# A graph layer with row gathers: 32 single rows per step instead of 40, one register load per engine and block, 43 fillers instead of 42

## The chip, the cores and the metric

The kernel runs on one core of one Trainium2 chip. The metric is the device time of one execution in microseconds (us), median of the runs. The engines are named PE (TensorE, matrix products), DVE (VectorE), ACT (ScalarE), POOL (GpSimd) and SP (SyncE); SP and ACT here also issue transfers (DMAs), and POOL issues the indirect ones that gather rows by a list of indices.

## What is computed

One layer of a graph network over 50,000 nodes of 128 features and 1,650,000 edges, which come sorted by their target `dst`. 50,000 of the edges are self-loops, one for each node.

```
Xs = X[src]
m_data = Xs @ W_data.T + b_data
m_ctrl = Xs @ W_control.T + b_control
msg = where(edge_types == 0, m_data, m_ctrl)
agg = segment_sum(msg, dst, num_segments=N)
out = relu(agg + X @ W_self.T + b_self)
result = layernorm(x + out)
```

Since the products are linear, the kernel first sums the rows `x[src]` of each target and edge type, and multiplies the sums by the weights afterwards. So the large part of the work is to fetch 1,650,000 rows of 512 bytes and to add them up.

## The kernel before

**Blocks and steps.** The edges are cut into `NBLK` blocks, worked through one after the other by a loop over `b` that is unrolled by hand (L614 to L664). A block has `Q = 2` steps, and a step has three kinds of edges:

- `SIZE = 1536` edges in `R = 12` columns of 128, one on each partition. One indirect DMA on POOL (L477) gathers one column: 128 rows. A block has 24 such gathers, in four passes of `PASS = 6`, each with a buffer `y` of its own out of `SLOTS = 10`.
- `F = 42` fillers. Self-loops among the 1,536 need no gather, since their rows lie in the window of node rows `xT` which the block loads anyway. `fill(b)` (L309) finds the first `F` self-loops of the step and puts `F` other edges in their places, so that the same gathers bring `F` more edges. It is all on DVE: comparisons, products and sums over 26 columns x `F` numbers (`m`, `new`, `v_new`, `old`, `by`, L319 to L338). The self-loops that were put out are added back by `left_out_columns`, `left_out_matrix`, `left_out_numbers` and `left_out_rows`. It needs `F` self-loops in each step; `find_bad` (L565) counts them on the chip, and where a step has fewer than `F` a second, general way of computing the whole layer runs after the first (`general`, L667).
- `S = 40` single rows, each fetched by an ordinary DMA of 512 bytes at an address out of a register: `TURNS = (20, 20)`, 20 for each step by SP and 20 by ACT (`single_rows`, L437). `offsets` (L430) has DVE turn indices into byte offsets (`at_x`, L435); a register load (L446) brings them into the engine's registers, `LOADS = 2` loads of 20 registers for each block and engine; then 20 DMAs follow each load (L451).

So a step covers 1,536 + 42 + 40 = 1,618 edges and a block 3,236. The first block takes 3,072 edges without fillers and single rows, then come as many full blocks as fit (508), and the last block takes the rest, 3,040 edges, again by plain gathers alone: 24 of them. That is `NBLK = 510` and 510 x 24 = 12,240 gathers. The last 96 rows are one shorter gather.

**What comes after the gathers.** PE waits for a pass (L484), then multiplies the gathered rows by one-hot matrices (`oh`, L412, with counts `cnt`, L420, from DVE), which adds them up into `acc` (L496). At the end of a step it takes the 40 single rows in one more product (L502), for which it waits in `rows_fetched` (L456). DVE adds `acc` to `sums` (L512), PE multiplies by the weights (`layer`, L527), DVE forms relu, residual and the moments of the norm (L541 to L546), ACT takes the root (`sd`, L551), DVE scales (L557, L559) and SP writes the rows out (L563).

**The order of the work.** Each engine works through its own instructions in the order of the program. Single rows are fetched two blocks ahead (`AHEAD = 2`), fillers five (`RAHEAD = 5`). At block `b`, ACT's order is: load of 20 registers and 20 rows for `b + 2`, the root of block `b - 1`, load and 20 rows for `b + 2`. SP's order is: the window `xT` of `b + 3`, load and 20 rows, load and 20 rows, the writing out of block `b - 1`. At every tenth block SP also loads the edge lists of the next ten (`load_edges`), a group; there are 51 groups. POOL has nothing but the gathers after its first two microseconds.

Of the kernel before, what the change touches and what calls it, by code (L numbers as in the profile page):

```python
# [36 lines left out]
Q = 2  # L37
PASS = 6
B = 112
C = R * Q  # L40
F = 42
TURNS = (20, 20)
S = sum(TURNS)
LOADS = 2
X = Q * S
R1 = R + 1
C1 = Q * R1
SIZES = [P] * R
SIZE = sum(SIZES)
CE = Q * SIZE  # L50
BE = CE + Q * F + X
NBLK = 2 + (E - CE) // BE
REST = E - CE - (NBLK - 2) * BE
REST_ROWS = [min(n, max(0, REST - q * SIZE - sum(SIZES[:r]))) for q in range(Q) for r, n in enumerate(SIZES)]
# [23 lines left out]
TBL = GROUPS * GB  # L78
# [3 lines left out]
def plain(b):  # L82

    return b == 0 or b >= NBLK - 1
# [6 lines left out]
def straight(ctx, tc, c, x, x_t, src_t, dst_t, etype_t, src_f, dst_f, etype_f, src_x, dst_first, first_p, out):  # L91
# [35 lines left out]
                   allow_small_or_imprecise_dtypes=True)  # L127
    FILL = Q * F + C1
    small = keep_ps.tile([P, 2 * W + F + 2 * FILL + 2], F32, name="small")
    num_ps, rank_no_ps = small[:, :2 * W], small[:, 2 * W:2 * W + F]  # L130
    lists = [small[:, 2 * W + F + i * FILL:][:, :FILL] for i in range(2)]
    sums_at = [small[:Q * F, 2 * W + F + 2 * FILL + i:][:, :1] for i in range(2)]

# [29 lines left out]
    def load_edges(g):  # L163
        t = eds.tile([1, GB * X], I32, name="one_g")
        nc.sync.dma_start(t, src_x[None, g * GB * X:(g + 1) * GB * X])
        one_g[g] = t
        loads[g] = {}
        for name, a in (("s", src_t), ("d", dst_t), ("t", etype_t)):
            t = eds.tile([P, GB, C1], I32, name=name, bufs=1)
            nc.sync.dma_start(t.rearrange("p b c -> p (b c)"), a[:, g * GC:(g + 1) * GC])  # L170
            loads[g][name] = t
        for name, a in (("sf", src_f), ("df", dst_f), ("tf", etype_f)):
            t = eds.tile([GS, F], I32, name=name, bufs=1)
            nc.sync.dma_start(t, a[g * GS:(g + 1) * GS, :])
            loads[g][name] = t
# [54 lines left out]
    def check(d, rel, at, name):  # L230
        chk = eds.tile(list(d.shape), F32, name="chk" + name, bufs=1)
        nc.vector.scalar_tensor_tensor(chk, d, float(DST_PAD), rel, op0=ALU.is_lt, op1=ALU.mult)
        axes = AX.XY if len(d.shape) == 3 else AX.X
        nc.vector.tensor_reduce(at[0], chk, axes, ALU.min)
# [74 lines left out]
    def fill(b):  # L309
# [15 lines left out]
        v = fil.tile([P, C1], F32, name="v_new")  # L325
        nc.vector.tensor_reduce(v, new, AX.X, ALU.add)  # L326
        vi = fil.tile([P, C1], I32, name="vi")
# [9 lines left out]
        with nc.allow_low_precision(reason="whole numbers below 256, one of them not 0"):  # L337
            nc.vector.tensor_reduce(by, old.rearrange("p (q r) f -> p q f r", r=R1), AX.X, ALU.add)  # L338
        bys[b] = by
# [76 lines left out]
    def counts(b):  # L416

        cnt = ohp.tile([P, Q, 2 * W], BF16, name="cnt")
        with nc.allow_low_precision(reason="whole numbers up to R1"):
            nc.vector.tensor_reduce(cnt, ohs[b].rearrange("p (q r) w -> p q w r", r=R1), AX.X, ALU.add)  # L420
        cnts[b] = cnt
# [8 lines left out]
    def offsets(b):  # L430

        if not plain(b):
            g, i = divmod(b, GB)
            ats[b] = stp.tile([1, X], I32, name="at_x", bufs=AHEAD + 2)
            nc.vector.tensor_scalar(ats[b], one_g[g][:, i * X:(i + 1) * X], float(ROW), None, op0=ALU.mult)  # L435

    def single_rows(b, part):  # L437

        if part == 0:
            ys[b] = stp.tile([S, Q, D], F32, name="yx", bufs=ROW_SLOTS)  # L440
        both = []
        for j, (eng, dma) in enumerate(((SP, nc.sync), (ACT, nc.scalar))):
            n = Q * TURNS[j]
            k0, k1 = part * n // LOADS, (part + 1) * n // LOADS
            at = Q * sum(TURNS[:j])
            _, rows = nc.values_load_multi_w_load_instructions(ats[b][0:1, at + k0:at + k1], engines=[eng], **RANGE)  # L446
            both.append([(dma, fetched[j][b % ROW_SLOTS], *divmod(k0 + k, TURNS[j]), sum(TURNS[:j]), row)
                         for k, row in enumerate(rows)])
        for pair in zip_longest(*both):
            for dma, sem, q, k, at, row in filter(None, pair):  # L450
                copy = dma.dma_start(ys[b][at + k:at + k + 1, q, :].bitcast(U8), x_bytes[:, bass.ds(row, ROW)])  # L451
                copy.then_inc(sem, 16)
                tc.no_tile_sem_insts.add(copy.ins.name)
                tc.add_to_no_dep_group(f"single{b}", copy.ins)

    def rows_fetched(b):  # L456

        times = len(range(b % ROW_SLOTS or ROW_SLOTS, b + 1, ROW_SLOTS))
        for j in range(2):
            wait = nc.tensor.wait_ge(fetched[j][b % ROW_SLOTS], 16 * Q * TURNS[j] * times)  # L460
        tc.declare_fence(wait.ins, group=f"single{b}")
# [141 lines left out]
    for b in range(1, RAHEAD):  # L603
        fill(b)
        left_out_columns(b)
        left_out_matrix(b)
        if b < AHEAD:
            onehot(b)
            counts(b)
            for part in range(LOADS):  # L610
                single_rows(b, part)
        if b == 1:
            clear_sums()
    for b in range(NBLK + 1):  # L614
# [16 lines left out]
        for q, (step, ks) in enumerate(passes_of(b)):  # L631
# [26 lines left out]
            if q == 3:  # L658
                left_out_matrix(b + RAHEAD)
                offsets(b + AHEAD + 1)  # L660
            if q < LOADS and not plain(b + AHEAD):
                single_rows(b + AHEAD, q)
# [226 lines left out]
def gnn_resnorm(  # L889
# [50 lines left out]
    with ExitStack() as own:  # L940
        straight(own, tc, c, x, x_t, src_t, dst_t, etype_t, src_f, dst_f, etype_f, src_x,
                 dst_first, first_p, out)
# [58 lines left out]
```

## Time and profile before

| | |
|---|---|
| time before, median of 3 runs (lowest, highest) | 15340.11 us (15320.92, 15340.7) |
| the profiled execution's own time | 15323.45 us |
| its span, first to last instruction | 15321.7 us |
| POOL: gathers L477 with `idx` as list, 12,216 of them | 11540.9 us busy, 945 ns each |
| POOL: idle just before them | 3733.3 us |
| DVE busy | 10904.6 us, 71% of the span |
| PE busy (products; weight loads lie beside) | 8296.6 us, 54% |
| ACT busy (without the issuing of DMAs) | 153.6 us, 1% |
| one row's issue on SP or ACT: register move and DMA | 29 and 228 ns, 20,320 times on each |
| a load of 20 registers (L446), median | 1437 ns on ACT, 1378 ns on SP |

How to read it: an instruction's row gives its count, its mean duration, and how long its engine sat idle just before it, with what ended that idle time ("issue" where nothing that the profile shows was waited for). In the timeline each line has the start, the duration, the engine (ACTq, SPq and PEq are the sequencers that issue DMAs and wait), the line of the kernel, the operation and its tiles.

### The profile page before, as it was taken

The numbers are of one execution on the slowest core, as the hardware profiler recorded it, in microseconds if no ns is written. First come the engines' busy times: TensorE is split into PE (matmuls) and PEld (weight loads), VectorE is DVE, ScalarE is ACT, GpSimd is POOL, SyncE is SP. The second block draws the span as 40 slices with busy tenths as digits, with TensorE's granted clock in tenths as the row PEclk, the third lists the DMA queues.
The fourth block names the chain that finished last, engine by engine and source line by source line (L and its number), as shares of the span: only waits on it lengthen the run. The fifth ranks groups of instructions, "written<-read, shape, count | busy, mean of one in ns | idle before, by whom it ended". The sixth has DMA issues, their size and how long they took to land. (4 is left out here: it accounts for less than half of the span.)

```text
span 15321.7 us, 197234 instructions
## 1 busy us (share of the span) xinstructions
PE 8296.6 (54%) x35844; PEld 7096.5 (46%) x35845; DVE 10904.6 (71%) x13994; ACT 153.6 (1%) x516; POOL 11565.0 (75%) x12250
## 2 busy tenths in 40 slices
PE   3555555555555555555555555555555555555555
PEld 3444444444444444444444444444444444444444
DVE  8777777777777777777777777777777777777775
ACT  0000000000000000000000000000000000000000
POOL 7777777777777777777777777777777777777777
PEclk7555555555555555555555555555555555555555
DMA  2222222222222222222222222222222222222222
GB/s 65 62 61 62 61 62 61 62 62 61 62 61 62 61 62 61 62 61 62 62 60 62 61 62 61 62 62 61 61 62 62 61 62 61 62 61 62 62 61 56
DMA packets 649293, 939.07 MB, mean 61 GB/s; under 512 B 327756, under 2 KB 445487, under 8 KB 648034
## 3 DMA queue, kind: packets, MB, share of 16 engines
q0 software_dynamic: 391680, 802.93, 20.9%
q1 hardware_dynamic: 215276, 112.76, 2.9%
q10 hardware_dynamic: 41078, 10.68, 0.3%
q14 instruction: 968, 7.93, 0.2%
q8 instruction: 291, 4.77, 0.1%
HBM read 895.92 MB, written 29.42 MB: 60 GB/s over the span
## 5 line engine op out<-in xcount | busy, mean ns | idle before, releaser
L477 POOL DMA_INDIRECT y<-in_x,idx x12216 | 11540.9, 945 | 3733.3 <-issue 3552.2
L496 PE MATMUL acc<-oh,y 128*128 128x120 f32 x24480 | 5867.6, 429 | 5768.3 <-PEq L484 5767.8
L496 PEld LDWEIGHTS acc<-oh,y 128*128 128x128 f32 x24480 | 5313.7, 326 | 6190.7 <-PEq L484 6178.3
L420 DVE TENSOR_REDUCE cnt<-oh 128x240 bf16<-128x3120 f32 x510 | 2959.6, 5803 | 0.1
L541 DVE COPY h<-po 112x128 f32<-112x128 f32 x510 | 148.7, 292 | 2499.1 <-PE po L535 2407.5
L412 DVE TENSOR_TENSOR oh<-col,small 128x3120 f32<-128x3120 f32 x510 | 1719.5, 3372 | 0.0
L512 DVE TENSOR_TENSOR sums<-acc,sums 128x180 f32 x1020 | 352.2, 345 | 1393.1 <-PE acc L505 1236.0
L338 DVE TENSOR_REDUCE by<-old 128x84 bf16<-128x1092 f32 x508 | 1078.5, 2123 | 17.6
L502 PE MATMUL acc<-oh,yx 40*128 40x120 f32 x2032 | 777.4, 484 | 0.0
L345 PE MATMUL small<-ones_b,by 128*84 128x1 bf16 x508 | 117.4, 231 | 1191.1 <-DVE by L338 1191.1
L319 DVE TENSOR_TENSOR m<-rk,small 128x1092 f32<-128x1092 f32 x508 | 656.4, 1292 | 17.3
L322 DVE TENSOR_TENSOR new<-m,small 128x1092 f32<-128x1092 f32 x508 | 656.2, 1292 | 17.3
L326 DVE TENSOR_REDUCE v_new<-new 128x26 f32<-128x1092 f32 x508 | 655.8, 1291 | 17.3
L345 PEld LDWEIGHTS <-by 128*84 128x84 bf16 x508 | 74.3, 146 | 1267.3 <-DVE by L338 1267.2
L335 DVE TENSOR_TENSOR old<-m,small 128x1092 f32<-128x1092 f32 x508 | 652.3, 1284 | 0.0
L502 PEld LDWEIGHTS acc<-oh,yx 40*128 40x128 f32 x2032 | 497.5, 304 | 210.0 <-issue 205.3
L535 PE MATMUL po<-wmsgT,sums 128*112 128x128 f32 x2040 | 515.1, 396 | 0.0
L535 PEld LDWEIGHTS po<-wmsgT,sums 128*112 128x112 f32 x2040 | 374.0, 253 | 108.2 <-issue 88.7
L533 PE MATMUL po<-bias,sums 3*112 3x128 f32 x1020 | 350.3, 439 | 0.0
L525 DVE TENSOR_TENSOR sums<-pl,sums 128x336 f32<-128x336 f32 x508 | 257.9, 508 | 85.2 <-DVE sums L512 84.6
L532 PE MATMUL po<-wselfT,xT 128*112 128x128 f32 x1020 | 315.5, 412 | 0.0
L551 ACT ACTIVATE sd<-mv,eps 112x1 f32<-112x1 f32 x510 | 150.4, 295 | 15051.3 <-DVE mv L546 8335.5
(118 smaller groups left out, 4174.2 us busy)
## 6 DMA issues: line engine op xcount, KB each, us to landing
yx<-in_x ACTq DMA_DIRECT2D x20320, 0.5 KB
yx<-in_x SPq DMA_DIRECT2D x20320, 0.5 KB
y<-in_x,idx POOLq DMA_INDIRECT x12216
xT<-in_x_t SPq DMA_DIRECT2D x510, 56.0 KB
out<-o SPq DMA_DIRECT2D x510, 56.0 KB
vf_all<-vd SPq DMA_DIRECT2D x51, 420.0 KB
s<-in_src_t SPq DMA_DIRECT2D x51, 130.0 KB
d<-in_dst_t SPq DMA_DIRECT2D x51, 130.0 KB
```

What stands on the lines that cost most here:

```text
L319: nc.vector.tensor_tensor(m, rk_g[g][:, i, :, None].to_broadcast([P, C1, F]), rank_no_ps[:, None, :].to_broadcast([P, C1, F]), op=ALU.is_e ...
L322: nc.vector.tensor_tensor(new.rearrange("p (q r) f -> p q r f", r=R1), m.rearrange("p (q r) f -> p q r f", r=R1), vf.rearrange("p (q f) -> ...
L326: nc.vector.tensor_reduce(v, new, AX.X, ALU.add)
L335: nc.vector.tensor_tensor(old, m, cb[:, :, None].to_broadcast([P, C1, F]), op=ALU.mult)
L338: nc.vector.tensor_reduce(by, old.rearrange("p (q r) f -> p q f r", r=R1), AX.X, ALU.add)
L412: nc.vector.tensor_tensor(oh, col_g[g][:, i, :, None].to_broadcast([P, C1, 2 * W]), num_ps[:, None, :].to_broadcast([P, C1, 2 * W]), op=AL ...
L420: nc.vector.tensor_reduce(cnt, ohs[b].rearrange("p (q r) w -> p q w r", r=R1), AX.X, ALU.add)
L477: copy = nc.gpsimd.indirect_dma_start(out=y[:r, k % PASS, :].bitcast(U8), out_offset=None, in_=x_rows, in_offset=bass.IndirectOffsetOnAxis ...
L496: nc.tensor.matmul(acc[:, :2, :].rearrange("p t w -> p (t w)"), y[:r, k % PASS, :], ohs[b][:r, column(k), :], start=k == of_step[0], stop= ...
L502: nc.tensor.matmul(acc[:, :2, :].rearrange("p t w -> p (t w)"), ys[b][:, q, :], ohs[b][:S, q * R1 + R, :], start=False, stop=True)
L512: nc.vector.tensor_tensor(part, accs.pop((b, q)), part, op=ALU.add)
L535: nc.tensor.matmul(po, a[:, t, :B], c["wmsgT"][:, t * D:(t + 1) * D], start=False, stop=t == 1)
```

## The change

The numbers of single rows, loads and fillers change, and with them the cut of the edges. `BEGIN` is the place in `at_x` where each engine's offsets begin, rounded up to four; `part_of` cuts a block's offsets into `LOADS` parts.

```diff
-F = 42
-TURNS = (20, 20)
+F = 43
+TURNS = (16, 16)
 S = sum(TURNS)
-LOADS = 2
-X = Q * S
+LOADS = 1
+BEGIN = (0, -(-Q * TURNS[0] // 4) * 4)
+X = BEGIN[1] + -(-Q * TURNS[1] // 4) * 4
...
-BE = CE + Q * F + X
+BE = CE + Q * (F + S)
 NBLK = 2 + (E - CE) // BE
...
+    def part_of(n, part):
+
+        return n if part == LOADS else -(-part * n // (4 * LOADS)) * 4
+
     def single_rows(b, part):
...
             n = Q * TURNS[j]
-            k0, k1 = part * n // LOADS, (part + 1) * n // LOADS
-            at = Q * sum(TURNS[:j])
+            k0, k1 = part_of(n, part), part_of(n, part + 1)
+            at = BEGIN[j]
             _, rows = nc.values_load_multi_w_load_instructions(ats[b][0:1, at + k0:at + k1], engines=[eng], **RANGE)
...
-        ones[1:] = np.concatenate([single[:, :, sum(TURNS[:j]):][:, :, :n].reshape(TBL - 1, Q * n)
-                                   for j, n in enumerate(TURNS)], axis=1)
+        for j, n in enumerate(TURNS):
+            ones[1:, BEGIN[j]:BEGIN[j] + Q * n] = single[:, :, sum(TURNS[:j]):][:, :, :n].reshape(TBL - 1, Q * n)
```

A step now covers 1,536 + 43 + 32 = 1,611 edges and a block 3,222. That makes 511 full blocks instead of 508, `NBLK = 513`, and leaves 486 edges for the last block: four gathers, the last of 102 rows. For each full block, SP and ACT now issue one load of 32 registers and 32 rows each, all of them ahead of ACT's root of the block before (with `LOADS = 1`, L661 calls `single_rows` at the first pass alone). `S = 32` rows enter the product L502 instead of 40. The groups become 52.

## The prediction

> **What bounds the kernel now.** I read the page's first parts to see which engine has least room, then the groups of instructions for that engine, then the timeline of one block for what its gaps are. The page:
>
> ```profile
> PE 8296.6 (54%) x35844; PEld 7096.5 (46%) x35845; DVE 10904.6 (71%) x13994; ACT 153.6 (1%) x516; POOL 11565.0 (75%) x12250
> ...
> L477 POOL DMA_INDIRECT y<-in_x,idx x12216 | 11540.9, 945 | 3733.3 <-issue 3552.2
> L496 PE MATMUL acc<-oh,y 128*128 128x120 f32 x24480 | 5867.6, 429 | 5768.3 <-PEq L484 5767.8
> L496 PEld LDWEIGHTS acc<-oh,y 128*128 128x128 f32 x24480 | 5313.7, 326 | 6190.7 <-PEq L484 6178.3
> ```
>
> No engine is above 75%, yet POOL's busy time and the idle time just before its gathers make 11540.9 + 3733.3 = 15274.2 us of the 15321.7. 3552.2 us of that idle time is "issue", a gap in which POOL waited for nothing shown: 0.30 us after every gather. PE's largest idle time is the wait for gathered rows (L484). So POOL issues gathers back to back, and everything else follows it. The timeline of one block, some lines of it:
>
> ```profile
> 7517.97 14.49 SPq L451 DMA_DIRECT2D yx<-in_x  x40
> ...
> 7518.98 0.95 POOL L477 DMA_INDIRECT y<-in_x,idx  x1 [0.30 <-issue]
> ...
> 7524.73 0.29 ACT L551 ACTIVATE sd<-mv,eps 112x1 f32<-112x1 f32 x1 [29.59 <-DVE mv L546]
> ...
> 7526.31 28.88 ACTq L451 DMA_DIRECT2D yx<-in_x  x40
> ...
> 7531.47 0.94 POOL L477 DMA_INDIRECT y<-in_x,idx  x1 [0.30 <-issue]
> ...
> 7533.96 0.94 POOL L477 DMA_INDIRECT y<-in_x,idx  x1 [0.30 <-issue]
> ...
> 7536.44 0.15 DVE L557 RECIPROCAL rstd<-sd 112x1 f32<-112x1 f32 x1
> ...
> 7546.41 0.26 DVE L435 TENSOR_SCALAR at_x<-one_g 1x80 int32<-1x80 int32 x1
> 7546.45 0.95 POOL L477 DMA_INDIRECT y<-in_x,idx  x1 [0.30 <-issue]
> ```
>
> Two things are to be seen. First, ten gathers lie between 7518.98 and 7531.47 and ten between 7533.96 and 7546.45: 1.249 us each in both stretches. In the first SP and ACT are issuing rows all the time; in the second they issue none. (ACT's line of 28.88 us merges two batches. The first ends near 7526.31 + 20 x 0.317 = 7532.7, as a row takes 0.317 us: 29 + 228 ns and two gaps of some 30. The second can't begin before `at_x` is written at 7546.67.) Second, SP and ACT stand idle for some 14 of the block's 30 us: the queues of the single rows bound nothing.
>
> The whole run agrees with this. The first gather, the first after the start-up, and the last:
>
> ```profile
> 3.21 1.12 POOL L477 DMA_INDIRECT y<-in_x,idx  x1 [1.09 <-DMA idx<-in_src_t]
> ...
> 85.50 0.94 POOL L477 DMA_INDIRECT y<-in_x,idx  x1 [3.19 <-PE acc L496]
> ...
> 15305.30 0.92 POOL L477 DMA_INDIRECT y<-in_x,s  x1 [0.30 <-issue]
> ```
>
> The one at 85.50 is the 61st, since POOL has buffers for 10 x 6 gathers and here waits for PE to free the first. From it to the last, the 12,240th, are 12,179 intervals in 15219.80 us: 1.2497 us each, 29.99 us per block of 24.
>
> **The change part by part.**
>
> *More gathers: +65.0 us, on the path.* Three more full blocks and a last block of four gathers instead of 24 make 24 + 511 x 24 + 4 = 12,292 gathers, 52 more. At 1.2497 us each that is 64.98 us. This is the cost of dropping 16 single rows per block: the rows that SP and ACT fetched beside POOL's work are now gathered by POOL. One more filler per step gives back only two of the sixteen.
>
> *Fewer rows and one load on SP and ACT: 0 on the path.* Per block and engine 8 rows x 0.317 = 2.5 us are saved, in queues that are idle for 14 us. What hides any cost is that idle time and, for the rows themselves, the two blocks between fetch and use. In the order of the work one thing moves: ACT's root now comes after 32 rows instead of 20, so 12 x 0.317 = 3.8 us later, plus what a load of 32 registers takes beyond one of 20. The trace has no load of 32. Bounds: nothing more than the 1.44 us of 20 registers (SP's five-register load L400 has a median of 1.29, so the number hardly counts there), or two loads of 20, 1.44 more. I take 0.9, 12 registers at 1.44/20 each. The root ends 3.8 to 5.3 us later. Behind it on DVE waits L557. In this block the root was done at 7524.73 + 0.29 = 7525.02 and L557 began at 7536.44, because the counts (L420, 5.8 us) come before it: 11.4 us of cover. Were the cover gone, DVE would stall and the writing out would be late, and only then, through `acc` and `sums`, PE and POOL's buffers. On SP all rows are issued in one batch and end earlier than the second batch of 20 did; the writing out L563 behind them waits for DVE anyway.
>
> The Trainium skill speaks against the longer load: "Runtime: NRT & Kernel Launch", section "Instruction fetch mechanics", puts a register load at about 200 ns per register. The row here says 72 ns (1437 / 20). By the page, 32 registers would take an estimated 6.4 us, the root would come some 8.8 us later, still within the 11.4, and the sum would stay the same.
>
> *43 fillers: +0.17 us of DVE per block, hidden; +0.7 us once.* L319, L322, L326, L335 and L338 go from 26 x 42 = 1,092 to 1,118 elements. Together they take 1292 + 1292 + 1291 + 1284 + 2123 = 7282 ns, and 26/1092 of it is 0.17 us. DVE waits per block 2499.1 / 510 = 4.9 us before L541 and 1393.1 / 510 = 2.7 before the 2 x L512, which covers it. At the start it isn't covered: four fills come one after the other before PE's first products, and the wait at 85.50 ends on them (PE's L345 at 82.20 waits for the fourth fill's L338, and L496 follows it): 4 x 0.17 = 0.7 us.
>
> *The end: +4.6 us.* Before, the last block's 24 gathers hid the previous block's layer. With four gathers (5 us) they don't. Lines of the end before:
>
> ```profile
> 15277.97 2.92 PE L496 MATMUL acc<-oh,y 128*128 128x120 f32 x12 [4.45 <-PEq L484]
> ...
> 15283.78 0.39 DVE L523 COPY sums<-sums 128x336 f32 x1 [0.16 <-DVE sums L512]
> ...
> 15307.88 2.92 PE L496 MATMUL acc<-oh,y 128*128 128x120 f32 x12 [4.33 <-PEq L484]
> ...
> 15313.44 0.29 DVE L541 COPY h<-po 112x128 f32<-112x128 f32 x1 [2.16 <-PE po L535]
> ...
> 15315.22 0.34 DVE L559 TENSOR_SCALAR o<-h,mv,rstd 112x128 f32<-112x128 f32 x1
> ```
>
> From the last gather's start at 15305.30: products begin 2.6 us later, and L559 ends at 10.3. After the change: products of the last four gathers from 2.6 to 4.5 (two thirds of 2.9), counts to 4.9, then the previous block's layer (2.7 us, L531 to L535 here) to 7.6, its moments, root and scaling (2.1 us, 15313.44 to 15315.56) to 9.8, the last `acc` into `sums` to 10.5, the bias and weight products that need it (2.1) to 12.7, moments, root and scaling (2.1) to 14.9: 4.6 us more. Bounds: 0, if these stages overlap fully, and 6, the previous block's layer, moments and scaling in full with the last `acc`.
>
> One more group (the ten-block loads) costs what it costs in the 1.2497 already. Sum: 15323.45 + 65.0 + 0.7 + 4.6 = 15393.8 us against the profiled execution. Two of the three runs shown, and the median, lie 17 us above that execution (15340.11 to 15323.45); with the same distance the median after is 15340.1 + 70.3 = 15410 us, 0.46% more. From the lowest run it would be 15391.
>
> **The rivals.**
>
> *Fewer row issues make POOL's gathers shorter, so that it is not slower.* For it: the rows share memory and DMA engines with the gathers, and 0.30 of every 1.25 us is an unexplained gap. Against: the two stretches above, 1.249 with and without rows. To cancel 70 us, the 12,231 intervals after the start-up would have to shrink by 5.7 ns, to 1.244; that is the shortest gather (940 ns, against 944 in the median) with its gap of 0.30. At 1.240 for all, the median would be 15410 - 12231 x 0.0097 = 15291 us.
>
> *Something late reaches POOL.* A root, or rows, later than their cover. It decides from 11.4 us of extra lateness at ACT's root on; each microsecond per block that gets through costs 511 us, so one would give 15,920. Against it: 3.8 to 5.3.
>
> *The second, general computation runs.* `find_bad` asks for F self-loops in each step. Counted in the reference's edges, cut as the changed kernel cuts them, the 1,022 steps with fillers hold at least 43, which is just enough for `least < F` to be false. If a count were short, the general part's 400 x 35 gathers alone would add 14,000 x 1.25 = 17,500 us: some 32,900.
>
> **How the numbers follow.** The forecast has 0.92, shorter gathers 0.04 (half of it past no change), a late wait 0.03, the general part 0.01. The likeliest is 15410. Its terms' bounds give 65 to 72 above a median that may itself fall at the low or the high run (15321 to 15341): 15386 to 15413; I widen the upper side to 15428 for a pitch 1 ns longer (12 us). About 0.2% (31 us) is what a measurement of this kernel can tell from no change. Slower has 0.92 + 0.03 + 0.01 = 0.96, within it 0.02, faster 0.02: even with the lowest level after against the median before, the forecast is 51 us slower.
>
> **What would show it.** Right: 12,292 gathers with the same 945 ns and 0.30 gap; idle before L477 of about 3733 + 52 x 0.30 = 3750; span about 15392; the last gather's start some 66 us later; rows on SP and ACT 511 x 32 = 16,352 each. ACT's root about 4 us later against L557, with no new wait at L557. Wrong: a pitch other than 1.2497 us, POOL waiting for PE or DVE inside the run, or L557 waiting for ACT.

## The result and the profile after

The changed kernel takes 15410.52 us, median of five runs (15410.25 to 15412.33), against 15340.11 before (15320.92 to 15342.42, five runs as well). The ratio is 1.0048 [1.0034, 1.0063]: slower by 70 us. The profiled execution took 15410.25 us, its span is 15408.5.

The code has moved by one to five lines: the gathers L477 are now L482, PE's products L496 and L502 are L501 and L507, the rows L451 are L456, the register load L446 is L451, the root L551 is L556, the reciprocal L557 behind it L562 and the scaling L559 L564. From the page of the changed kernel, the engines, the costliest groups and the row transfers of SP:

```profile
PE 8332.6 (54%) x36022; PEld 7121.3 (46%) x36023; DVE 11046.6 (72%) x14092; ACT 154.4 (1%) x519; POOL 11631.0 (75%) x12302
...
L482 POOL DMA_INDIRECT y<-in_x,idx x12288 | 11625.6, 946 | 3755.3 <-issue 3584.1
L501 PE MATMUL acc<-oh,y 128*128 128x120 f32 x24584 | 5887.9, 429 | 5743.0 <-PEq L489 5742.6
...
yx<-in_x SPq DMA_DIRECT2D x16352, 0.5 KB
```

POOL's gathers and the idle time before them are still nearly the whole span: 11625.6 + 3755.3 = 15380.9 of 15408.5 us. Their number is the forecast one (12,288 in this group and four with shorter or other lists make 12,292), and so is the idle time of 3755 us, of which nearly all is the gap of 0.30 us after each gather. The timeline of one block of the changed kernel shows the rows and the root:

```profile
7524.57 0.17 DVE L436 TENSOR_SCALAR at_x<-one_g 1x64 int32<-1x64 int32 x1
...
7526.92 10.71 SPq L456 DMA_DIRECT2D yx<-in_x  x32
7527.08 10.66 ACTq L456 DMA_DIRECT2D yx<-in_x  x32
...
7537.85 0.29 ACT L556 ACTIVATE sd<-mv,eps 112x1 f32<-112x1 f32 x1 [29.84 <-PE acc L501]
...
7544.52 0.15 DVE L562 RECIPROCAL rstd<-sd 112x1 f32<-112x1 f32 x1
```

Both engines issue 32 rows in one stretch of 10.7 us and none in the rest of the 30 us. The root ends at 7538.14, and DVE asks for it at 7544.52: 6.4 us of cover are left of 11.4. The 61st and the last gather, and what comes behind the last, in the same timeline:

```profile
85.84 0.95 POOL L482 DMA_INDIRECT y<-in_x,idx  x1 [3.54 <-PE acc L501]
...
15387.00 1.10 POOL L482 DMA_INDIRECT y<-in_x,s  x1 [0.30 <-issue]
...
15390.13 2.04 PE L501 MATMUL acc<-oh,y 128*128 128x120 f32 x8 [1.15 <-PEq L489]
...
15401.21 0.34 DVE L564 TENSOR_SCALAR o<-h,mv,rstd 112x128 f32<-112x128 f32 x1
```

From the 61st to the last, the 12,292nd, are 12,231 intervals in 15301.16 us: 1.2510 us each, against 1.2497 in the profile of before. Behind the last gather's start lie 21.5 us, against 16.4 before.

So of the 86.8 us between the two profiled spans, 52 x 1.2497 = 65.0 are the added gathers, 0.3 the start and 5.1 the end. The other 16 are 12,231 intervals that are each 1.3 ns longer. That is about as much as separated the profile of before (15323.45) from its own median. The kernel before has executions near 15321 and near 15340 us; such a value is called a level here. Two things had to be tried: whether those 1.3 ns belong to the changed kernel or to the level on which a run lies, and whether the 70 us between the medians are the 52 gathers or the new work per block.

### The profile page after: what moved, and what is told of

Same layout as the page of the kernel before. It is cut to its first block, busy times and chain, and to the rows that moved or that the text cites. A ratio compares the mean times of both kernels' runs of the same rounds, so it can differ in the third digit from the quotient of the medians.

```text
span 15408.5 us, 180949 instructions
## 1 busy us (share of the span) xinstructions
PE 8332.6 (54%) x36022; PEld 7121.3 (46%) x36023; DVE 11046.6 (72%) x14092; ACT 154.4 (1%) x519; POOL 11631.0 (75%) x12302
## 3 DMA queue, kind: packets, MB, share of 16 engines
q0 software_dynamic: 393376, 806.34, 20.8%
## 4 chain that ended last, share of the span: by engine, by line
POOL 49%; issue 18%; PE 14%; DVE 12%; DMA 7%; PEldq 0%; POOLq 0%; DVEq 0%; ACTq 0%; SPq 0%; ACT 0%; PEld 0%
POOL y L482 49%; PE acc L501 8%; DMA y<-in_x,idx 6%; DVE cnt L421 3%; PE po L540 2%; PE po L538 2%; DVE by L339 1%; PE po L537 1%; DVE m L320 1%; DVE new L323 1%; DVE v_new L327 1%; DVE old L336 1%; DVE h L546 1%; DVE h L547 1%; PE po L536 0%
## 5 line engine op out<-in xcount | busy, mean ns | idle before, releaser
L482 POOL DMA_INDIRECT y<-in_x,idx x12288 | 11625.6, 946 | 3755.3 <-issue 3584.1
L501 PE MATMUL acc<-oh,y 128*128 128x120 f32 x24584 | 5887.9, 429 | 5743.0 <-PEq L489 5742.6
L501 PEld LDWEIGHTS acc<-oh,y 128*128 128x128 f32 x24584 | 5332.5, 326 | 6166.8 <-PEq L489 6160.3
L339 DVE TENSOR_REDUCE by<-old 128x86 bf16<-128x1118 f32 x511 | 1106.9, 2166 | 17.7
L346 PE MATMUL small<-ones_b,by 128*86 128x1 bf16 x511 | 118.2, 231 | 1269.5 <-DVE by L339 1269.5
L507 PE MATMUL acc<-oh,yx 32*128 32x120 f32 x2044 | 780.2, 482 | 0.0
L346 PEld LDWEIGHTS <-by 128*86 128x86 bf16 x511 | 74.8, 146 | 1346.9 <-DVE by L339 1346.9
L320 DVE TENSOR_TENSOR m<-rk,small 128x1118 f32<-128x1118 f32 x511 | 674.4, 1320 | 17.4
L323 DVE TENSOR_TENSOR new<-m,small 128x1118 f32<-128x1118 f32 x511 | 674.4, 1320 | 17.5
L327 DVE TENSOR_REDUCE v_new<-new 128x26 f32<-128x1118 f32 x511 | 673.2, 1317 | 17.5
L336 DVE TENSOR_TENSOR old<-m,small 128x1118 f32<-128x1118 f32 x511 | 670.0, 1311 | 0.0
L507 PEld LDWEIGHTS acc<-oh,yx 32*128 32x128 f32 x2044 | 498.2, 302 | 211.6 <-issue 206.8
L556 ACT ACTIVATE sd<-mv,eps 112x1 f32<-112x1 f32 x513 | 151.2, 295 | 15131.0 <-PE acc L501 8570.7
```

Of the source, the lines that this page charges most:

```text
L320: nc.vector.tensor_tensor(m, rk_g[g][:, i, :, None].to_broadcast([P, C1, F]), rank_no_ps[:, None, :].to_broadcast([P, C1, F]), op=ALU.is_e ...
L323: nc.vector.tensor_tensor(new.rearrange("p (q r) f -> p q r f", r=R1), m.rearrange("p (q r) f -> p q r f", r=R1), vf.rearrange("p (q f) -> ...
L336: nc.vector.tensor_tensor(old, m, cb[:, :, None].to_broadcast([P, C1, F]), op=ALU.mult)
L482: copy = nc.gpsimd.indirect_dma_start(out=y[:r, k % PASS, :].bitcast(U8), out_offset=None, in_=x_rows, in_offset=bass.IndirectOffsetOnAxis ...
L501: nc.tensor.matmul(acc[:, :2, :].rearrange("p t w -> p (t w)"), y[:r, k % PASS, :], ohs[b][:r, column(k), :], start=k == of_step[0], stop= ...
L507: nc.tensor.matmul(acc[:, :2, :].rearrange("p t w -> p (t w)"), ys[b][:, q, :], ohs[b][:S, q * R1 + R, :], start=False, stop=True)
```

## The experiments

Times of a kernel are compared with the kernel before on the same chip. In the decompositions below, "interval" is the mean distance of gather starts from the 61st to the last, and "gather" their mean duration, both from the trace.

**The kernel before again.** No edit; it asks for the level.

> The kernel before, unchanged. Theory: its two levels of time (15321 and 15340 us) are two lengths of a gather on POOL (944.6 ns on average in the profiled execution of before, 946.0 in the one of after), so a profile at 15340 us has gathers of 946.0 ns and an interval between gathers of 1.2510 us instead of 1.2497. Rival: the longer gather is the change's doing (its buffers or its rows), and the kernel before has 944.6 ns at both levels.

Measured: 15333.39 us (15321.4 to 15335.77), ratio 1.0 [0.9991, 1.0009]. Again the first execution lay low, at 15321.4, the others at 15332 to 15336, and it was the first that was profiled. Its interval is 1.24954 us and its gather 944.43 ns, much as in the first profile of before (1.24968 and 944.58). So this run doesn't answer the question, since no profile of the kernel before at its higher level came about, here or later.

**The change's work per block on the old cut.** It keeps 32 rows, one load of 32 and 43 fillers, on the 508 full blocks of before. Seven edges of each step are left out for that, so what it computes is not the whole layer; the work of every engine in a block is that of the changed kernel.

```diff
-BE = CE + Q * (F + S)
+LEFT = 7
+BE = CE + Q * (F + S + LEFT)
...
-        steps = rest.reshape(TBL - 1, Q, SIZE + F + S)
+        steps = rest.reshape(TBL - 1, Q, SIZE + F + S + LEFT)[:, :, :SIZE + F + S]
```

> All of the changed work per block (43 fillers, 16 + 16 single rows, one load of 32 registers), but the blocks keep the old length: 7 edges of each step are left out, so there are 510 blocks and 12,240 gathers as before. Theory (only the number of gathers counts): 15340 us, the same as before within 2 us, +0.7 at most. Rival (the work per block on SP, ACT or DVE counts too, or fewer rows make gathers shorter): 15320 or less, or 15400 or more.

Measured: 15336.6 us (15334.45 to 15338.12) beside 15333.63 for the kernel before on that chip: +3.0, ratio 1.0002 [0.9993, 1.0011]. Nothing that can be told from no change: fewer rows, the longer load, the later root and the 43rd filler together are worth a few us at most, and not the 70.

**The old work on the new cut.** The counterpart: 40 rows, two loads of 20 and 42 fillers, but blocks of 3,222 edges; seven of the 40 rows of each step are empty ones.

```diff
-BE = CE + Q * F + X
+EMPTY = 7
+BE = CE + Q * (F + S - EMPTY)
...
-        steps = rest.reshape(TBL - 1, Q, SIZE + F + S)
+        steps = rest.reshape(TBL - 1, Q, SIZE + F + S - EMPTY)
+        steps = np.concatenate([steps, np.full((TBL - 1, Q, EMPTY), pad, np.int32)], axis=2)
```

> All of the old work per block (42 fillers, 20 + 20 single rows, two loads of 20 registers), but the blocks are cut as in the changed kernel, 3,222 edges: the last 7 single rows of each step are empty (they fetch row 0 and are not added). 513 blocks, 12,292 gathers. Theory: the changed kernel's time, 15410 us. Rival: near 15340 us, if the time came from the work per block.

Measured: 15403.27 us (15402.94 to 15405.06), +69.6, ratio 1.0046 [1.0032, 1.006]. The cut alone, with the old work on every engine, costs what the whole change costs. The two together settle where the 70 us come from: 52 gathers and an end that four gathers don't cover.

**Two loads of 16.** The change with two loads for each block and engine, so that ACT's root comes after 16 rows again.

```diff
-LOADS = 1
+LOADS = 2
```

> The changed kernel with two loads of 16 registers instead of one of 32, the root between the two batches as before; 12,292 gathers. Theory (the load and the place of the root are hidden): 15410 us as the changed kernel, with the root ending some 4 us earlier against L562. Rival (the later root costs something): 15400 us or less.

Measured: 15410.59 us, ratio 1.005 [1.0036, 1.0064], 77 above the kernel before. The shorter load and earlier root bring nothing. It is even 7 us above the run before it, and the trace says where: what the gathers of more than 960 ns take beyond the mean of the others sums to 19.7 us, against 10.6 to 12.6 in the profiles of before, of the changed kernel and of the three runs above. They lie where DVE works out the columns of the next group (`columns`, once in each group): 18.2 of the 19.7 us belong to gathers that begin within 10 us of the start of that work, and 8.4 to 10.6 us in the other profiles. The lists themselves are loaded some 90 us earlier, and no long gather stands within 6 us of that. Why they were longer here was not found. It also gave the price of a load of 16. The instructions of L451 on ACT (count, then least, median and greatest duration in ns), first the changed kernel's, then this run's:

```profile
L451 ACTq TENSOR_LOAD <-at_x x511: 2106/2122/2266, 16.6 to 15289.7; - x171
```

```profile
L451 ACTq TENSOR_LOAD <-at_x x1022: 1177/1195/1347, 16.2 to 15309.5; - x171
```

16 registers take 1195 ns and 32 take 2122: 58 ns for each further one, 0.27 us for the load itself. 20 had taken 1437.

**More rows instead of fewer.** If rows cost nothing while SP and ACT have room, the change goes the wrong way, and more rows should make the kernel faster until one of the two queues is full. Four kernels took the edit to the other side: 64 rows per step with 43 fillers, 68 with 42, then 72 and 80 with 43. Against the changed kernel, for 64 rows, for 68, and for 72 (for 80 with `TURNS = (40, 40)`):

```diff
-TURNS = (16, 16)
+TURNS = (32, 32)
...
-LOADS = 1
+LOADS = 2
```

```diff
-F = 43
-TURNS = (16, 16)
+F = 42
+TURNS = (34, 34)
...
-LOADS = 1
+LOADS = 3
```

```diff
-TURNS = (16, 16)
+TURNS = (36, 36)
...
-LOADS = 1
+LOADS = 3
```

> The other direction: 64 single rows per step, 32 each by SP and ACT, in two loads of 32 registers per block and engine; 43 fillers; 503 blocks, 12,054 gathers, 186 fewer than before. Theory: 186 x 1.251 = 233 us less, about +3 for a last block of 6 gathers: 15110 us. Per block ACT needs some 2 x 0.6 + 64 x 0.375 + 0.35 = 25.5 us of 30, so POOL still bounds. Rival (SP and ACT were closer to the bound than their idle time says, or more rows slow the gathers): 15250 us or more.

> 68 single rows per step, 34 by each, three loads of 24, 24 and 20 registers; 42 fillers; 502 blocks, 12,032 gathers. Theory: 15340 - 208 x 1.251 + 3 = 15083 us, as SP needs 68 x 0.379 + 1.8 + 1.5 = 29.1 us of 30. Rival (SP's group loads, 3 us in every tenth block, push it over): 15110 us or more, with POOL waiting for PE.

> 72 single rows per step, 36 by each, three loads of 24 registers; 43 fillers; 500 blocks, 11,996 gathers. By POOL alone 15340 - 244 x 1.251 + 2 = 15037 us. Theory: here SP becomes the bound, 72 x 0.379 + 1.8 + 1.5 = 30.6 us per block, so 500 x 30.6 = 15300 us, and POOL waits. Rival (POOL still bounds): 15037 us.

> 80 single rows per step, 40 by each, three loads of 28, 28 and 24 registers; 43 fillers; 498 blocks, 11,938 gathers, 14,967 us by POOL alone. Theory: SP bounds clearly, 80 x 0.379 + 1.8 + 1.5 = 33.6 us per block, 16,740 us, and POOL idles for buffers. Rival: under 15,100 us.

Beside 15322.17 us for the kernel before on this chip:

| rows per step | gathers | time, us | ratio | interval, us | gather, ns |
|---|---|---|---|---|---|
| 64 | 12,054 | 15108.62 | 0.986 [0.9844, 0.9877] | 1.2507 | 945.5 |
| 68 | 12,032 | 15072.07 | 0.9836 [0.982, 0.9853] | 1.2502 | 944.9 |
| 72 | 11,996 | 16013.75 | 1.0451 [1.0434, 1.0468] | 1.3309 | 944.7 |
| 80 | 11,938 | 17406.71 | 1.1359 [1.134, 1.1378] | 1.4546 | 944.6 |

64 and 68 do as forecast: the interval stays at 1.25 us, so that gathers left out are time gained. With 64, 186 fewer are 232 us, and 214 came: the intervals are 1.2 ns longer than in the low profiles of before (14 us; the gathers of over 960 ns take 22.5 us beyond the others' mean), and the end is 5 us longer. With 68, 208 fewer are 260 us, and 250 came. With 68 the kernel is 250 us faster than before, the best version found. From 72 on a gather is as long as ever, but POOL no longer issues them back to back, and the mean gap grows from 305 to 386 and 510 ns. The waits of the kernel with 68 rows and of that with 72 (who waits, for what: us in all, times, longest us):

```profile
POOL y L482 <- issue: 3548.3, 11622, 0.3
...
POOL y L482 <- PE acc L501: 23.3, 67, 3.2
...
PE acc L507 <- PEq L465: 2710.5, 403, 16.5
```

```profile
PE acc L507 <- PEq L465: 3627.3, 422, 22.3
...
POOL y L482 <- issue: 3339.1, 10935, 0.3
...
POOL y L482 <- PE acc L501: 1073.7, 410, 11.5
```

With 68 rows PE already waits 2710 us for single rows (L465), but this is hidden: POOL's waits for PE sum to 23.3 us, and but for the one of 3.2 us at the start none is longer than the usual gap. With 72 PE's wait of 3627 us reaches through its products to POOL's buffers: 410 waits, 1073.7 us, up to 11.5 us each. 72 and 80 came out slower than expected (16,014 and 17,407 us against 15,300 and 16,740), as a block took 32.0 and 35.0 us instead of 30.6 and 33.6. At least a part of it is a wait that the sum over rows and loads left out. SP's waits with 72 rows:

```profile
SPq L175 <- DMA out<-o: 528.6, 48, 12.6
```

Before it loads the lists of a new group SP, which has no time to spare now, stands 528.6 / 48 = 11.0 us for a result to be written out; over some 500 blocks that is about 1 us per block. (With 68 rows the same wait came to 360.1 us, and POOL was not late for it.)

**A third pair, and 70 rows, on another chip.** The change and the kernel before, unchanged, to see both on a new chip, and 35 rows each on SP and ACT to find the edge between 68 and 72 (against the changed kernel):

```diff
-F = 43
-TURNS = (16, 16)
+F = 42
+TURNS = (35, 35)
...
-LOADS = 1
+LOADS = 3
```

> The changed kernel as it is, beside the kernel before on one chip. Theory: whatever level this chip has, the difference is 52 gathers at this run's interval (65.0 us) and about 5 us at the end, 70 us in all. Rival (the work per block adds something of its own, as the two loads of 16 lay 7 us above the old work in the new cut): 77 us.

> The kernel before once more, for a profile on the same chip as the changed one. Theory: gathers of the same length in both profiles (bar those over 960 ns) where the two kernels run at the same level, so that the difference is in their number. Rival: gathers of the changed kernel are over 1 ns longer than these.

> 70 single rows per step, 35 by each, three loads of 24, 24 and 22 registers; 42 fillers; 501 blocks, 12,018 gathers. By POOL alone 222 gathers fewer than before, 278 us less, so some 2 us of the end apart 0.982 of the time of before. Theory: SP needs per block 70 x 0.379 + 1.8 + 1.5 = 29.8 us of 30.0, and its loads for a group of ten blocks (3 us) push it over, so POOL waits and the ratio is above the 0.9836 of 68 rows. Rival: 0.982.

Measured: of this only the equal gathers came out, 945.9 ns in both profiles without those over 960 ns. On this chip the kernel before takes 19,223.25 us (19,165.69 to 19,296.72, 17 runs) and 19,226.89 in the second of these runs; the change takes 18,233.02, ratio 0.9484 [0.9467, 0.95]; 70 rows take 25,058.98, ratio 1.3039 [1.3013, 1.3065]. Here the change is *faster* by 5%, and more rows are far slower. The same groups as in the page above, first of the kernel before on this chip, then of the changed one:

```profile
L477 POOL DMA_INDIRECT y<-in_x,idx x12216 | 11564.6, 947 | 7603.3 <-issue 3334.0
...
L502 PE MATMUL acc<-oh,yx 40*128 40x120 f32 x2032 | 636.9, 402 | 5237.7 <-PEq L460 3323.9
```

```profile
L482 POOL DMA_INDIRECT y<-in_x,idx x12288 | 11639.5, 947 | 6545.8 <-issue 3350.1
...
L507 PE MATMUL acc<-oh,yx 32*128 32x120 f32 x2044 | 619.2, 365 | 459.3 <-issue 458.1
```

A gather takes 947 ns, 1 or 2 more than in the pages above, but 7603 us of idle time lie before the gathers instead of 3733, and PE's product with the single rows, which waited for nothing before, waits 3324 us for them. In the changed kernel that wait is gone. So the single rows hold up the kernel before on this chip. The reason is in the instructions that issue them. Register moves and DMAs of the rows on SP, kernel before on this chip (least, median and greatest ns):

```profile
L451 SPq MOVE yx<-in_x x20320: 1/29/1468, 28.1 to 19226.3; - x200
L451 SPq DMA_DIRECT2D yx<-in_x x20320: 1/228/1478, 28.9 to 19226.4; - x200
```

The medians are those of the first profile, 29 and 228 ns, but the distance from one row's start to the next behind the same register load has a mean of 0.797 us on SP and 0.642 on ACT, against 0.332 and 0.338 in the first profile of before; 54% of SP's rows start more than 0.45 us after the one before, against 2%. The stalls come in steps of about 0.70 us. One of them seen from the other engines, in the timeline of the same run:

```profile
9020.02 13.42 SPq L451 DMA_DIRECT2D yx<-in_x  x16
...
9034.95 0.78 PE L502 MATMUL acc<-oh,yx 40*128 40x120 f32 x2 [20.80 <-PEq L460]
...
9039.29 0.95 POOL L477 DMA_INDIRECT y<-in_x,idx  x1 [11.22 <-PE acc L496]
```

Sixteen rows take 13.42 us instead of some 5; PE stands 20.8 us for single rows, and POOL then 11.2 us for the buffers that PE frees. Forty rows on SP at 0.797 us and two loads of 1.20 are 34.3 us per block, more than the 30 that the gathers take; in the changed kernel 32 rows at 0.850 and one load of 2.03 are 29.2.

Still the changed kernel's intervals are 1.4797 us on average here (the kernel before: 1.5698), and not 1.25. Among what comes late in it is the root, which stands behind all 32 rows on ACT. In the timeline of the changed kernel on this chip:

```profile
9010.76 21.20 ACTq L456 DMA_DIRECT2D yx<-in_x  x32
...
9019.36 0.26 PE L501 MATMUL acc<-oh,y 128*128 128x120 f32 x1 [1.16 <-issue]
...
9032.06 0.30 ACT L556 ACTIVATE sd<-mv,eps 112x1 f32<-112x1 f32 x1 [34.92 <-issue]
...
9032.39 0.16 DVE L562 RECIPROCAL rstd<-sd 112x1 f32<-112x1 f32 x1 [2.00 <-issue]
```

DVE's L562 begins as soon as the root is done: it stands idle before it 381 times in the run, 969 us, against 14 times and 67 us in the kernel before on this chip. PE is hit by the stalls too, as its product at 9019.36 shows, before which it waits 1.16 us for nothing shown; of the pairs of products L510 the second begins more than 0.45 us after the first in 37%, in the changed kernel's last run below in none. In the chain of work that ended last, ACT's rows (L456) make 18.6% of the span. The changed kernel takes some 2,800 us more here than in that last run; how they divide between the late root, PE's stalls and the rest was not measured. What makes the engines stall on this chip was not found. The edge between 68 and 72 rows on the other chips stays open too, since 70 ran only here.

**The change once more,** on a fourth chip, for the pair that the run before failed to give.

> The changed kernel once more beside the kernel before, since the last job's chip ran both in another regime (before at 19,223 us, SP and ACT stalling between rows in steps of 0.70 us, POOL waiting for rows). Theory: where SP and ACT issue a row in 0.317 us, the difference is 70 us (52 gathers and the end), 0.46%; where they stall, the change is faster, as it has fewer rows. Rival: the two loads' 7 us in the run with 16 + 16 rows belong to the changed work per block, so that 77 us are measured.

Measured: 15393.42 us (15392.51 to 15394.86) beside 15322.39 (15320.77 to 15323.06): +71.0, ratio 1.0047 [1.0033, 1.0061]. That is the theory's 70 and not the rival's 77, so the 7 us more of the two loads of 16 are not part of the change. Now the changed kernel lies at a low level, and so it can be set against the kernel before at the same level. The 61st and the last gather of the kernel before (its second profile), then those of this run, in the timeline:

```profile
85.43 0.94 POOL L477 DMA_INDIRECT y<-in_x,idx  x1 [3.18 <-PE acc L496]
...
15303.55 0.92 POOL L477 DMA_INDIRECT y<-in_x,s  x1 [0.30 <-issue]
```

```profile
85.53 0.94 POOL L482 DMA_INDIRECT y<-in_x,idx  x1 [3.57 <-PE acc L501]
...
15369.29 1.09 POOL L482 DMA_INDIRECT y<-in_x,s  x1 [0.31 <-issue]
```

15218.12 / 12,179 = 1.24954 us and 15283.76 / 12,231 = 1.24959: the change leaves the interval alone to within 0.05 ns. The 71.1 us between the two spans (15390.8 and 15319.7) are 52 x 1.2496 = 65.0 for the gathers, 0.1 for the start, 0.7 for the interval and 5.4 for the end. This is called the clean pair below.

## Why the prediction was right

The mechanism and the large sizes held where both kernels were first timed and on three of the four chips of the experiments; on the other one a premise fell. That the forecast of 15410 us met the measured 15410.52 so closely is in part luck, as the points on the start, the end and the level show.

- *52 more gathers at 1.2497, +65.0.* Right: 12,292 gathers, and 65.0 of the 71.1 us in the clean pair. The cut alone gave +69.6.
- *Fewer rows and the longer load, 0.* Right on the ordinary chips: the whole new work per block made +3.0, which is not to be told from nothing. The load of 32 takes 2.12 us on ACT, 0.2 less than the estimate of 1.44 + 0.9. By the rule of the Trainium skill ("Runtime: NRT & Kernel Launch", "Instruction fetch mechanics", about 200 ns for each register) an estimated 6.4 us were to be expected. That section speaks of the register loads that the runtime puts in around a kernel, which no run here shows; for this kernel's own loads the measurement of 58 ns per further register decides. In the block shown the root's cover shrank from 11.4 to 6.4 us, 5.0 against a forecast of 3.8 to 5.3. Over all blocks the median of this cover is 6.2 us, against 11.0 before. L562 waited for the root in two cases of the whole run, 0.8 us together (before in one, 0.4).
- *43 fillers.* 0.15 us of DVE per block against 0.17 forecast (1320 + 1320 + 1317 + 1311 + 2166 ns make 7434, before 7282), and hidden. The once-only cost at the start was mis-sized: 0.1 us in the clean pair and 0.34 between the first two profiles, not 0.7.
- *The end, +4.6.* Measured 5.4 in the clean pair and 5.1 between the first two profiles. The products of the last four gathers begin 3.1 us after the last one's start and not 2.6, as PE waits for the rows until then (1.15 us). The last scaling ends 14.6 us after it, against 14.9 in the working; so the rest of the difference lies behind the scaling, in what closes the run.
- *The level, +17.* Right in its effect, without a reason given for it: the profiled execution lay 17 us below the median before and at the median after. So the first profile after shows what the prediction had named as signs of being wrong, an interval of 1.2510 us instead of 1.2497 and a span of 15408.5 instead of 15392, and only the clean pair shows the signs of being right: 1.24959 us, 15390.8, and a last gather 65.7 us later. (The upper end of the range, 15428, is 3 us more than its own terms give, 15413 + 12.) What a level is, the gather's duration shows. Without those above 960 ns, the mean gather is 943.5 to 943.6 ns in both profiles of before at 15320 us and in the changed kernel at 15393, 944.5 to 944.7 in the three runs of the new cut or the new work beside the repeat of before, and 944.9 in the changed kernel at 15410. It is constant through a run and the gap stays at 305 ns; 1.3 ns on 12,231 gathers are 16 us. The changed kernel has both values, so that the level belongs to the run and not to the change. That the kernel before at 15340 has longer gathers is concluded from this, since it was never profiled there; that it can have them is shown by the chip of the stalls, where it and the changed kernel both have 945.9 ns. What sets the level was not found.
- *The rival of shorter gathers* fell: same gather, same gap, with 32, 40, 64 and 68 rows.
- *The rival of the second computation* fell: the run has the 12,292 gathers forecast and no others.
- *The rival of something late at POOL* fell for the root on the ordinary chips. On the one other chip it came true in both kernels: in the kernel before the single rows were late, and in the changed one the root, whose cover there is gone in most blocks (381 waits of L562 in 513 blocks). The change, by issuing fewer rows, still took back 990 us. The prediction took 0.317 us per row and "idle for some 14 of the block's 30 us" as properties of the kernel. They held on every chip but that one.

## What to carry to other kernels

Where one engine issues the same instruction back to back, the time is their number times its interval: work that moves away from it pays in full as long as the queues that take it have room, and work that moves back costs in full, however much it relieves them. The room has a sharp end, though, here between 34 rows per step and engine (0.9836) and 36 (1.045), so it is worth adding up everything that a queue does in a block, its waits too. Room in a queue is also cover against a chip on which that queue is slower: 40 rows were 0.5% better than 32 where the queues ran as in the first profile, and 5% worse on the one chip where they stalled. And an instruction that stands behind a whole batch in such a queue, as the root does in the changed kernel, is late with it.

## What the hardware showed that was not expected

- The duration of the same gather differs by run or chip, constant through a run: 943.3 to 945.9 ns on average without those over 960. Over 12,000 of them that is some 30 us, 0.2% of the time.
- On one chip the instructions of SP, ACT and PE came in steps of about 0.70 us and its multiples (54% of SP's rows in the kernel before more than 0.45 us after the one before, elsewhere 2%), while a gather took 947 ns there and its usual gap was the 0.30 us of elsewhere; the kernel before went from 15,322 to 19,223 us.
- Most of what gathers of over 960 ns (up to 1.20 us) took beyond the others' mean stood beside DVE's work on the columns of a group: 10.6 of 12.1 us in the first profile of before, 18.2 of 19.7 with two loads of 16. The cause stays open.
- A register load took 1.195, 1.437 and 2.122 us for 16, 20 and 32 registers on ACT: about 58 ns for each and 0.27 for the load.
